# Two-layer block, its attention: on which queue the turned probabilities are read back from DRAM

## The chip, the core and the metric

The kernel runs on one core of one Trainium2 chip, in one launch. The metric is the time of that launch on the device in microseconds, as the median of several runs. All data are float32.

## The reference, cut to what matters

The program computes two transformer-like layers over `x` of shape (4, 512, 512). Before each sublayer `x` goes through a gate, a bidirectional scan over the sequence (`bi_wkv`), and each sublayer's result is added to `x`. Layer 0 is a state-space mixer and a mixture of 8 experts, layer 1 an attention and a gated feed-forward net (FFN).

```python
x = x + mamba2(gate0(x));  x = x + moe(gate1(x))
x = x + attention(gate2(x));  x = x + ffn(gate3(x))

def attention(x, w_q, w_kv, w_dense):      # 16 heads in 4 groups, 128 channels each
    q = (x @ w_q).reshape(b, 512, 4, 4, 128)
    k, v = split(x @ w_kv)                 # one k and one v for each group of 4 heads
    s = einsum('bqgpd,bkgd->bqgpk', q, k) * 128 ** -0.5
    p = softmax(where(causal, s, -inf))
    ctx = einsum('bqgpk,bkgd->bqgpd', p, v)
    return ctx.reshape(b, 512, 2048) @ w_dense
```

## The kernel before

The kernel is written for a scheduling layer: the program states its operations in an order, the layer puts them on the engines' queues in an order of its own choice and adds the semaphores. `tc.issue_after(i)` ties what is written inside it behind instruction `i` in that order. The helper `after(*engines)` (L88) does that with the last instruction so far of each engine named.

Every queue works in its own order. TensorE runs matrix products; VectorE (DVE), ScalarE (ACT) and GpSimd (POOL) run elementwise work; SyncE (SP) only issues DMA transfers. A DMA is issued by one of the engines' queues. The issuing queue first waits for what the transfer needs, and whatever stands behind it on that queue waits too.

The attention runs over `heads_` (L1738): four groups `g`, in each four batches `b`, in each four heads `i`, so 64 heads. I count them 0 to 63 in that order; the four heads of one (`g`, `b`) are called first to fourth. For one head:

- `start_group` (L1585), once in four heads: `pk` (L1593) and `pv` (L1601) on TensorE, copied by ScalarE to `kT` (L1597) and `v` (L1609).
- `queries` (L1612): `pq` (L1615) on TensorE, scaled to `qT` (L1623) by ScalarE. `begin(n + 1)` writes it one head ahead.
- `scores` (L1626), for each of four blocks of 128 queries (`qi`): `psc` (L1637) on TensorE; mask (L1640) and negated maximum `nmax` (L1642) on VectorE; the exponential `pr` with its row sum on ScalarE (`act`, the helper's line L128); reciprocal and scaling (L1648, L1649) and `nc.vector.transpose` (L1653) on VectorE. That last turns each 32x32 square and writes it to `blocks`.
- `blocks` (one of two `turned` tiles) then lies with its 32x32 squares in the wrong places among the partitions. Four transfers on GpSimd's queue (L1661) write it to a DRAM buffer `d`, one of four in turn. One transfer (L1678, in `collect`) reads it back as `pT`, all squares in place: 128 partitions of 1,664 elements. `pT` has two buffers.
- `context` (L1682): `pctx` (L1703) on TensorE with `pT` and `v`, copied by ScalarE to `cx` (L1711). After the fourth head `dense` (L1714) runs `pd` (L1718) and adds to `x` on VectorE (L1726).

The loop (L1757) holds three heads back: `context` of head n - 3 is written after `scores` of head n. `collect(1)` is called in `scores`, ahead of the first block (L1635). It reads back the blocks of all heads but the newest one written. So the readback of head n - 2 is written at the start of head n's scores, behind `qT` of head n + 1. `collect()` within `context` takes what is left; that happens only for head 61, since heads 62 and 63 are turned on TensorE (`ptp`, L1690) and do not go through DRAM. 62 heads are read back.

Beside the heads VectorE and ScalarE compute gates for later sublayers, in pieces. `nudge` (L390) steps that generator, four times a head, under `with after(nc.vector, nc.scalar)` (L1643). The gates' inputs come on SyncE's queue: `kt` (L240), `ek` (L247), `ekv` (L249), and their results leave there (L344). Also on SyncE's queue are the experts' result rows `rr` (L1483, `combine`), the weights `wq`, `wkv`, `wd` (L1466, L1472, L1566) and the FFN's weights (L1834 to L1839). ScalarE's queue issues only the 16 output transfers of the FFN (L1828).

Of the kernel before, what the change touches and what calls it, by code (L numbers as in the profile page):

```python
# [83 lines left out]
def block_kernel(ctx: ExitStack, tc: tile.TileContext, a: dict, out: bass.AP):  # L84
    nc = tc.nc

    @contextmanager
    def after(*engines):  # L88

        with ExitStack() as es:  # L90
            for e in engines:
                last = next(
                    (i for i in reversed(nc.cur_bb.bb.instructions) if i.engine == e.engine), None
                )
                if last is not None:
                    es.enter_context(tc.issue_after(last))
            yield
# [1454 lines left out]
    with att as ph:  # L1552
# [73 lines left out]
        def scores(u, i, qT):  # L1626
# [5 lines left out]
            for qi in range(NT):  # L1632
                n = (qi + 1) * P
                if qi == 0:
                    collect(1)  # L1635
                psc = ps_mm("psc")
                nc.tensor.matmul(  # L1637
                    psc[:, :n], lhsT=qT[:, qi * P : n], rhs=u.kT[:, :n], start=True, stop=True
                )
                nc.vector.tensor_tensor(psc[:, qi * P : n], psc[:, qi * P : n], mask, ALU.add)  # L1640
                nmax = sm.tile([P, 1], F32, tag="nmax", name="nmax", bufs=4)
                nc.vector.tensor_reduce(nmax, psc[:, :n], AX.X, ALU.max, negate=True)  # L1642
                with after(nc.vector, nc.scalar):  # L1643
                    nudge()
                pr = sm.tile([P, n], F32, tag=f"pr{qi}", name="pr")
                rsum = sm.tile([P, 1], F32, tag="rsum", name="rsum", bufs=4)
                act(pr, psc[:, :n], AF.Exp, bias=nmax, accum_out=rsum)
                nc.vector.reciprocal(rsum, rsum)  # L1648
                nc.vector.tensor_scalar(pr, pr, rsum, None, ALU.mult)  # L1649
                if turn:  # L1650
                    prs.append(pr)
                    continue
                nc.vector.transpose(  # L1653
                    blocks[:, :, 3 * qi : 4 * qi + 1, :].rearrange("p c k j -> p k c j"), pr
                )
# [14 lines left out]
        def new_pT():  # L1670
            return sm.tile([P, QUAD, SLOTS, SQ], F32, tag="pT", name="pT")

        def collect(rest=0):

            while len(away) > rest:
                d = away.pop(0)
                back[id(d)] = pT = new_pT()
                nc.sync.dma_start(  # L1678
                    out=pT.rearrange("p r k j -> p (r k j)"), in_=d.rearrange("c i r s -> (c i) (r s)")
                )  # L1680

        def context(u, prs):  # L1682

            if isinstance(prs, list):
                pT = new_pT()
                for qi, pr in enumerate(prs):
                    n = (qi + 1) * P
                    ptp = ps_tp("ptp")
                    for kj in range(qi + 1):
                        nc.tensor.transpose(  # L1690
                            ptp[:, kj * P : (kj + 1) * P], pr[:, kj * P : (kj + 1) * P], ident
                        )
                    nc.any.tensor_copy(
                        pT[:, :, 3 * qi : 4 * qi + 1, :].rearrange("p r k j -> p k r j"),
                        ptp[:, :n].rearrange("p (k r j) -> p k r j", r=QUAD, j=SQ),
                    )
            else:
                if id(prs) not in back:
                    collect()
                pT = back.pop(id(prs))  # L1700
# [86 lines left out]
    with ExitStack() as ph:  # L1787
# [48 lines left out]
        for lo, hi in ((0, 4), (4, 8), (8, NFF)):  # L1836
            nc.sync.dma_start(
                out=wdn[:, lo:hi, :],
                in_=ffd_d[lo * P : hi * P, :].rearrange("(i p) m -> p i m", p=P),  # L1839
# [44 lines left out]
        with tc.If(n_odd > 0):  # L1884
            with ExitStack() as gen:
                wl = gen.enter_context(tc.tile_pool(name="ff_gen", bufs=2, **right))
                for b in range(B):
                    h = gated(3, b, x[b], gp, tag="h", name=f"h4_{b}")
                    hd = []
                    for i in range(NFF):  # L1890
                        cs = slice(i * P, (i + 1) * P)
                        pv = []
                        for name in ("gateT", "upT"):
                            w = wl.tile([P, NC, P], F32, tag=name, name=name)
                            nc.sync.dma_start(
                                out=w, in_=a[name][:, cs].rearrange("(k p) m -> p k m", p=P)
# [13 lines left out]
                    for m in range(NC):  # L1910
                        w = wl.tile([P, NFF, P], F32, tag="downT", name="downT")
                        nc.sync.dma_start(
                            out=w,
                            in_=a["downT"][:, m * P : (m + 1) * P].rearrange("(i p) m -> p i m", p=P),
# [76 lines left out]
```

## Time and profile before

| what | value |
|---|---|
| runs shown | 2270.66, 2264.39, 2270.62 us, median 2270.62 |
| the profiled execution | 2262.92 us, of which the span is 2260.9 |
| granted TensorE clock in it | 0.983 of full speed |
| TensorE busy | 2123.0 us, 94% of the span |
| VectorE busy | 1524.8 us, 67% |
| ScalarE busy | 971.5 us, 43% |
| GpSimd busy | 418.4 us, 19% |
| readback issues (L1678) | 62 on SyncE's queue, 832 KB each, from 1171.4 to 1972.4 us |
| write issues (L1661) | 248 on GpSimd's queue, 208 KB each, 4.0 us from issue to landing (median) |

The profile is one execution with a record of each instruction's start and length and of each DMA packet. The span goes from its first instruction to its last; the profiled execution's own time is 2.0 us longer. Some engines wait beside others' work, so a wait counts only where it stands on the path to the end. A wait is put down to what ended it. "SPq" and "ACTq" are the queues of SyncE and ScalarE, where issuing a DMA is not counted as busy time. The attention's heads lie between some 1143 and 2003 us.

### The profile page before, as it was taken

The page shows a single profiled execution, that of the slowest core. Times are in us where ns is not written, and L with a number is a line of the kernel's source. Part 1 is how long each engine was busy: PE and PEld are TensorE (multiplying, and loading weights), DVE is VectorE, ACT ScalarE, POOL GpSimd, SP SyncE. Part 2 cuts the span into 40 slices and gives each one's busy share as a digit, 9 for nine tenths or more (in the row PEclk, how much of TensorE's full clock was granted, in tenths as well). Part 3 has the DMA queues.
Part 4 walks back from the last instruction along what each step waited for, and adds up shares of the span by engine and source line. Part 5 has one row for each costly group of instructions (what it writes and reads, how often), then busy time and mean ns, then how long its engine had stood idle before and what let it go on. Part 6 is the DMA issues. An engine that isn't in the chain of part 4 may idle for free.

```text
span 2260.9 us, 23897 instructions
## 1 busy us (share of the span) xinstructions
PE 2123.0 (94%) x7528; PEld 1219.8 (54%) x7528; DVE 1524.8 (67%) x3040; ACT 971.5 (43%) x1901; POOL 418.4 (19%) x558
## 2 busy tenths in 40 slices
PE   2879999999999999999989999999999999999998
PEld 1545565555655444444444555545555555568887
DVE  8698989989643665566577767677767765465332
ACT  4476676766732234333154433333334333243221
POOL 4023242321331111211211111111111111100000
PEclk9889999999999999999989999999999999999999
DMA  7542241531523548978666555455545464441100
GB/s 261 174 141 75 95 166 66 169 111 63 193 71 135 192 159 297 352 261 292 210 238 206 177 181 168 140 164 185 169 151 164 147 196 133 148 158 38 38 19 20
DMA packets 112455, 357.38 MB, mean 158 GB/s; under 512 B 14595, under 2 KB 23171, under 8 KB 102915
## 3 DMA queue, kind: packets, MB, share of 16 engines
q1 hardware_dynamic: 87584, 277.26, 36.1%
q0 software_dynamic: 22432, 74.34, 11.0%
q10 hardware_dynamic: 2304, 4.20, 0.5%
q8 instruction: 62, 1.02, 0.2%
q14 instruction: 73, 0.57, 0.1%
HBM read 337.91 MB, written 108.00 MB: 197 GB/s over the span
## 4 chain that ended last, share of the span: by engine, by line
PE 36%; DVE 9%; DMA 2%; ACT 2%; issue 1%; SPq 0%; DVEq 0%; ACTq 0%
PE pd L1718 9%; PE pq L1615 5%; PE pctx L1703 3%; PE psc L1637 3%; PE pk L1593 3%; PE pv L1601 3%; PE pfo L1821 2%; PE pfo L1820 2%; PE pfg L1820 2%; PE pfg L1821 2%; PE pfu L1821 2%; PE pfu L1820 2%; DVE turned L1653 2%; DVE nmax L1642 2%; DMA pT<-turned 1%; DVE pr L1649 1%
## 5 line engine op out<-in xcount | busy, mean ns | idle before, releaser
L1661 POOL DMA_DIRECT2D turned<-turned x248 | 135.2, 552 | 701.2 <-DVE turned L1653 399.0
L1615 PE MATMUL pq<-h,wq 128*128 128x512 f32 x512 | 230.9, 593 | 2.2 <-DVE h L404 1.7
L1718 PE MATMUL pd<-cx,wd 128*128 128x512 f32 x512 | 224.0, 593 | 1.9 <-ACT cx L1711 1.6
L128 ACT ACTIVATE pr<-psc,nmax 128x128 f32<-128x128 f32 (+3 forms) x256 | 134.6, 526 | 166.1 <-DVE nmax L1642 165.4
L1048 PE MATMUL pc<-h,wxb 128*128 128x512 f32 x320 | 148.5, 620 | 42.8 <-DVE h L1307 38.9
L1640 DVE TENSOR_TENSOR psc<-psc,mask 128x128 f32<-128x128 f32 x256 | 70.7, 284 | 144.3 <-PE psc L1637 144.3
L1637 PE MATMUL psc<-kT,qT 128*128 128x128 f32 (+3 forms) x512 | 156.3, 442 | 12.0 <-ACT pr L128 12.0
L1718 PEld LDWEIGHTS pd<-cx,wd 128*128 128x128 f32 x512 | 95.6, 190 | 118.5 <-issue 108.1
L1703 PE MATMUL pctx<-pT,v 128*128 128x512 f32 (+3 forms) x512 | 149.7, 434 | 9.9 <-DMA pT<-turned 9.6
L1703 PEld LDWEIGHTS pctx<-pT,v 128*128 128x128 f32 x512 | 96.6, 190 | 90.2 <-issue 61.1
L1615 PEld LDWEIGHTS pq<-h,wq 128*128 128x128 f32 x512 | 92.6, 190 | 96.3 <-issue 90.8
L811 PE MATMUL pg<-w,hT 128*128 128x512 f32 x296 | 136.6, 603 | 6.8 <-ACT hT L784 6.8
L844 PE MATMUL po<-w,yT 128*128 128x512 f32 x296 | 135.9, 600 | 6.2 <-ACT yT L837 6.2
L822 PE MATMUL pn<-w,hT 128*128 128x512 f32 x296 | 133.4, 593 | 0.0
L1048 PEld LDWEIGHTS pc<-h,wxb 128*128 128x128 f32 x320 | 61.9, 198 | 115.8 <-issue 73.8
L1642 DVE TENSOR_REDUCE nmax<-psc 128x1 f32<-128x128 f32 (+3 forms) x256 | 122.7, 482 | 2.1
L1637 PEld LDWEIGHTS psc<-kT,qT 128*128 128x128 f32 x512 | 85.9, 192 | 70.5 <-ACT pr L128 26.9
L1726 DVE TENSOR_TENSOR xr<-xr,pd 128x512 f32<-128x512 f32 x64 | 43.5, 680 | 117.7 <-PE pd L1718 117.7
L1653 DVE STREAM_TRANSPOSE turned<-pr 128x128 f32<-128x128 f32 x248 | 120.7, 498 | 1.8
L1119 PE MATMUL pz<-wzt,h 128*128 128x512 f32 x256 | 115.2, 599 | 0.3 <-ACT st L1220 0.3
L1267 PE MATMUL po<-wot,yT 128*128 128x512 f32 x256 | 114.2, 600 | 0.0
L811 PEld LDWEIGHTS pg<-w,hT 128*128 128x128 f32 x296 | 56.2, 194 | 75.9 <-issue 66.3
(343 smaller groups left out, 4172.9 us busy)
## 6 DMA issues: line engine op xcount, KB each, us to landing
w<-in_w1x SPq DMA_DIRECT2D x76, 1024.0 KB
turned<-turned POOLq DMA_DIRECT2D x248, 208.0 KB, 4.0
pT<-turned SPq DMA_DIRECT2D x62, 832.0 KB
w<-in_w2x SPq DMA_DIRECT2D x38, 1024.0 KB
wb<-in_b1x SPq DMA_DIRECT2D x38, 512.0 KB
lm<-cs SPq DMA_DIRECT2D x32, 512.0 KB
kt<-in_fT SPq DMA_DIRECT2D x62, 256.0 KB
ek<-ek SPq DMA_DIRECT2D x62, 256.0 KB
```

The costliest lines, as they stand in the source:

```text
L811: nc.tensor.matmul(pg, lhsT=hT[:, k, :], rhs=self.w1[s][0][:, k, :], start=(k == 0), stop=(k == NC - 1))
L844: nc.tensor.matmul(po, lhsT=yT[:, j, :], rhs=self.w2[s][:, j, :], start=(j == 0), stop=(j == NI - 1))
L1048: nc.tensor.matmul(pc, lhsT=wxb[:, k, m * P : (m + 1) * P], rhs=h[:, k, :], start=(k == 0), stop=(k == NC - 1),)
L1615: nc.tensor.matmul(pq, lhsT=u.wq[:, k, i * KVC : (i + 1) * KVC], rhs=u.h[:, k, :], start=(k == 0), stop=(k == NC - 1),)
L1637: nc.tensor.matmul(psc[:, :n], lhsT=qT[:, qi * P : n], rhs=u.kT[:, :n], start=True, stop=True)
L1642: nc.vector.tensor_reduce(nmax, psc[:, :n], AX.X, ALU.max, negate=True)
L1653: nc.vector.transpose(blocks[:, :, 3 * qi : 4 * qi + 1, :].rearrange("p c k j -> p k c j"), pr)
L1661: nc.gpsimd.dma_start(out=d[:, :, r].rearrange("c i s -> i c s"), in_=blocks[r * SQ : (r + 1) * SQ].rearrange("i c k j -> i c (k j)"),)
L1703: nc.tensor.matmul(pctx[:, kj * P :].rearrange("p (q r j) -> p q r j", r=QUAD, j=SQ), lhsT=u.v[:, kj, :], rhs=pT[:, :, 4 * kj : 10 + kj : ...
L1718: nc.tensor.matmul(po, lhsT=dense_w[u.g][:, i, m * P : (m + 1) * P], rhs=u.ctxT[i], start=(i == 0), stop=(i == HPG - 1),)
L1820: nc.tensor.matmul(out_, lhsT=w, rhs=xs[0], start=first_, stop=False)
L1821: nc.tensor.matmul(out_, lhsT=w, rhs=xs[1], start=False, stop=last_)
```

## The change

The readback in `collect` is issued on ScalarE's queue in place of SyncE's, and it is written under `after(nc.scalar)`, that is, tied behind the last instruction that was written for ScalarE before it. The bytes moved, the buffers and the writes on GpSimd's queue are the same. Lines below it move down by two.

```diff
             while len(away) > rest:
                 d = away.pop(0)
                 back[id(d)] = pT = new_pT()
-                nc.sync.dma_start(
-                    out=pT.rearrange("p r k j -> p (r k j)"), in_=d.rearrange("c i r s -> (c i) (r s)")
-                )
+                with after(nc.scalar):
+                    nc.scalar.dma_start(
+                        out=pT.rearrange("p r k j -> p (r k j)"),
+                        in_=d.rearrange("c i r s -> (c i) (r s)"),
+                    )
```

A DMA issued on ScalarE's queue is an instruction of ScalarE to `after`. The `nudge` that follows `collect` in the first block of a head is therefore tied behind the readback's issue, where before it was tied behind `qT` or a later ScalarE instruction.

## The prediction

> **What bounds the kernel now.** The page comes first. Its profiled execution took 2262.92 us, 2260.9 of them span. The runs shown have a median of 2270.62 (2264.39 to 2270.66), so I work out a difference against the profiled execution and add it to the median. A measurement of this kernel can tell about 0.3% (6.8 us) from no change.
>
> ```profile
> span 2260.9 us, 23897 instructions
> PE 2123.0 (94%) x7528; PEld 1219.8 (54%) x7528; DVE 1524.8 (67%) x3040; ACT 971.5 (43%) x1901; POOL 418.4 (19%) x558
> ```
>
> TensorE is the bound; ScalarE is less than half busy. Second, the table by stretches of the span, for the attention (columns: length; PE, PEld, DVE, ACT, POOL busy with counts; granted clock; DMA share; GB/s):
>
> ```profile
> 1120.00:1300.00 180.00, 161.47 (x552) 87.24 (x553) 129.71 (x309) 83.77 (x173) 28.84 (x54) 0.96 0.65 205
> 1300.00:1600.00 300.00, 289.20 (x926) 154.51 (x924) 213.27 (x556) 118.50 (x283) 50.05 (x92) 1.00 0.56 169
> 1600.00:2010.00 410.00, 405.04 (x1308) 218.88 (x1309) 250.02 (x686) 141.52 (x354) 61.01 (x113) 1.00 0.52 166
> ```
>
> TensorE is idle for 18.5 + 10.8 + 5.0 = 34.3 us of the 890. No change to the attention alone can win more than that, and after 1600 us almost nothing is left. Third, the chain of waits, TensorE's in the attention and SyncE's own in the whole span:
>
> ```profile
> PE psc L1637 <- ACT pr L128: 12.0, 12, 3.2
> PE pctx L1703 <- DMA pT<-turned: 9.6, 4, 3.3
> ...
> SPq L240 <- DVE eu L278: 243.0, 38, 20.5
> SPq L1678 <- DMA turned<-turned: 146.9, 40, 9.1
> ...
> SPq L1678 <- PE pctx L1703: 104.6, 11, 20.0
> ```
>
> The readback (L1678) reaches TensorE's clock by 9.6 us in 4 waits. The 251.5 us that SyncE stands at it cost nothing in themselves. They could only hurt through what is queued behind them, the gate loads (L240, L247, L249), and no engine's wait for those loads stands among TensorE's or VectorE's waits in the attention.
>
> Fourth, the timeline around the longest of the four waits, head 19 (heads count from 0 in the loop's order), SyncE, then ScalarE, then TensorE:
>
> ```profile
> 1429.26 0.33 SPq L240 DMA_DIRECT2D kt<-in_fT  x1
> 1429.81 0.82 SPq L1678 DMA_DIRECT2D pT<-turned  x1
> ...
> 1430.22 0.58 ACT L128 ACTIVATE pr<-psc,nmax 128x384 f32<-128x384 f32 x1 [0.42 <-DVE nmax L1642]
> ...
> 1438.07 2.39 PE L1703 MATMUL pctx<-pT,v 128*128 128x512 f32 x8 [3.31 <-DMA pT<-turned]
> ```
>
> The written blocks of head 19 had landed at 1424.9, but the readback was issued only at 1429.81, just behind a gate load that had waited for a buffer. It landed 7.8 us later, and TensorE lost 3.31. The other three waits look the same (heads 15, 23, 31: a gate load 0.56 us ahead in the queue). This is what the change goes for.
>
> **The removed part.** 62 issues of 0.32 us and their waits leave SyncE's queue. Gate, weight and row loads behind them start earlier. I price that at nothing: TensorE's waits that a load could shorten in the attention are `pcb` behind `rr` (4.4 us, 5 times), and those rows were held by a buffer that `pcb` itself frees. The FFN's weights leave the readbacks behind too and start before 1972 us, but TensorE has no wait for them to lose; their DMA then runs beside the last readbacks, which have 2 to 5 us to spare.
>
> **The added part: issuing on ScalarE.** The nearest row is the output's DMA, the one kind that ScalarE issues before:
>
> ```profile
> 2058.71 0.60 ACT L1806 CAST h_hi<-h 128x512 fp32r<-128x512 f32 x1
> 2058.83 0.38 ACTq L1828 DMA_DIRECT2D out<-ot  x1
> 2059.43 0.63 ACT L128 ACTIVATE th<-xr 128x512 f32<-128x512 f32 x1
> ```
>
> The issue goes out 0.12 us after the cast ahead of it starts, 0.48 before that cast ends, and the next instruction starts 0.12 after the cast's end (2058.71 + 0.60 = 2059.31). So an issue that need not wait costs ScalarE 0.12 us, or 0.34 where nothing covers it: 62 x 0.12 = 7 us, at most 62 x 0.34 = 21 us, on an engine that is idle for 546 of these 890 us. On the path only the 12 waits of TensorE for `pr` count: 12 x 0.12 = 1.4 at the low end, 12 x 0.34 = 4 at the high; below nothing too if the new order shortens them. I take +1.
>
> **The added wait.** ScalarE now stands at a readback until the head's four writes have landed. Queued behind it are the exponentials, `qT`, `kT`, `v` and `cx`, for which TensorE waits. For each of the 62 I took the ScalarE instruction that stands just ahead in the new built order, and compared its end in this trace with the landing of the last write. In 59 cases the writes had been down for 1.6 us or more before the issue. In the other three (heads 1, 13, 25) they are 0.7, 2.1 and 9.7 us short, but for 13 and 25 ScalarE's next TensorE-bound work, `kT`, starts only some 16 us later. Price: 0; from above, 3 us.
>
> [...]
>
> **The moved part: when the readback is issued.** The tie puts it behind the last ScalarE work written before it. In this trace's times that is a median of 4.2 us later than SyncE issued it, and 17 to 24 us later for most second heads of a group. What that costs, readback by readback: arrival is the end of the ScalarE instruction ahead less 0.48 (or the writes' landing, if later), plus the time this readback took in the trace from issue to its last 6,656-byte packet (3.9 to 8.5 us, median 5.1). Need is the start of its `pctx`, less its wait of before, plus the TensorE work that the new order puts ahead of it. Slack by place in the group of four:
> - first heads: 6 to 22 us. Dense and the next group's `pk`, `pv` lie between.
> - second heads: 1.3 us or more, but for head 61. That one is collected inside `context`, so behind `cx` of head 60: 1.8 short, with 2.9 us of transposes put between.
> - third heads: 3.1 or more, but for head 2 (0.5 short) and head 6 (0).
> - fourth heads: here it fails. Short are head 3 by 2.8, 15 by 1.5, 19 by 3.3, 23 by 2.7, 27 by 2.7, 31 by 2.9, 35 by 0.2, together 16.1.
>
> The sum is 16.1 + 1.8 + 0.5 = 18.4 us of waits, where 9.6 stood: +8.8. That keeps each transfer as slow as it was. The other end takes them at the undisturbed 4.1 us (head 51 issued at 1852.1, landed 1856.2): then short are only head 3 by 1.2, 27 by 0.3, 31 by 1.0, 61 by 1.9, in all 4.4, which is -5.2. The truth lies between. The gate load that ran just ahead on SyncE's queue now has a queue of its own, but the next head's writes (2.2 us of the 16 DMA engines beside head 19) stay. I take the middle, 11.4, so +1.8.
>
> [...]
>
> **Order on the other engines.** In the built order TensorE's rows stay in place but for some four dozen moves (`pq`, `pk` and the first `pctx` earlier or later by one to four matmuls); VectorE has several hundred, mostly gate scans against `nmax` and `rsum`, because the gate work is tied to the last ScalarE instruction, now a DMA. GpSimd's order is the same. VectorE waits for TensorE (144.3 us at `psc`), not the other way, after 1300 us. Before that, TensorE's 18.5 idle us can move either way; I take 0 and keep 5 on both sides.
>
> **The sum.** +1.8 waits for `pT`, +1 ScalarE, 0 the rest: 2262.9 + 2.8 = 2265.7 for a profiled execution like this one, and 2270.62 + 2.8 = 2273.4 for the median. I say 2273.5.
>
> **The rivals.**
> - Slower: the transfers stay as slow as they were on SyncE's queue, and fourth heads pay in full. +8.8, with ScalarE's high end 4 and its late landings 3: 2279 to 2287. For it: the later issue is in the built order, and the writes still overlap. Against it: one of the two causes of slow transfers is gone. It decides where a fourth head's readback takes over about 5 us. Chance 0.28.
> - Much slower: ScalarE becomes the head of the line. If VectorE's new order makes the last transposes of a head 5 us later, the 1.6 to 10 us by which fourth heads' writes precede are gone, and the exponentials behind stop: 15 fourth heads by 2 us and more, 2290 to 2310. Against it: 59 of 62 with margin. Chance 0.08.
> - Faster: all waits for `pT` fall (-9.6), and part of the early idle time, up to 5 us: 2257 to 2264. For it: four waits behind a gate load, which vanish in kind. Against it: ScalarE reaches the readback no earlier than SyncE did. Chance 0.22.
> - About the same, the forecast: 2263 to 2279. Chance 0.42.
>
> The range 2259 to 2288 leaves out the much slower case and the tails of the outer two. Faster by over 0.3% (under 2263.8) is the faster case: 0.22. Slower (over 2277.4) is the two slower cases and a little of the forecast: 0.38. Within 0.3%: 0.40.
>
> **What would show it.** TensorE's wait `pctx <- DMA pT<-turned` at 8 to 15 us in 6 to 9 waits, all at fourth heads and head 61; ScalarE's DMA rows of 0.34 us without long idle ahead of the next exponential; 4 to 6 us from issue to landing. If that wait is under 3 us, the faster rival holds; over 18, the slower. If `pr` waits for DMA, or TensorE's wait for `pr` goes well beyond 12.0, ScalarE is the head of the line. If the stretch 1120 to 1300 moves by over 5 us, the orders of VectorE and TensorE decided, which I priced at nothing.

## The result, and the profile after

The changed kernel takes 2287.34 us (median of 10 runs, 2280.01 to 2291.92) where the kernel before took 2269.18 (10 runs beside them, 2261.4 to 2277.68). The ratio is 1.0078, with a 95% interval of 1.0064 to 1.0092: slower by 18.2 us. The profiled execution took 2286.27 us, 1.1 below its median; that of before, 2262.92, lies 6.3 below its own. The head of the page after, and its chain of work that ended last, by engine:

```profile
span 2284.5 us, 23902 instructions
PE 2138.2 (94%) x7528; PEld 1230.4 (54%) x7528; DVE 1527.0 (67%) x3041; ACT 970.2 (42%) x1900; POOL 416.3 (18%) x558
...
PE 37%; DVE 8%; DMA 4%; ACT 1%; issue 1%; ACTq 0%; DVEq 0%; SPq 0%
```

TensorE's instruction count is the same, and its busy time is 15.2 us longer for those 7528 matmuls. The table by stretches has the first reason in its clock column:

```profile
1120.00:1300.00 180.00, 159.47 (x524) 84.82 (x523) 131.98 (x314) 84.41 (x174) 27.89 (x52) 0.95 0.66 212
1300.00:1600.00 300.00, 287.43 (x928) 155.34 (x927) 197.78 (x508) 107.08 (x259) 45.87 (x84) 0.98 0.53 161
1600.00:2010.00 410.00, 402.36 (x1284) 216.18 (x1283) 260.01 (x719) 141.98 (x360) 67.76 (x124) 1.00 0.53 160
```

Between 1300 and 1600 us the granted clock was 1.00 before and is 0.98 now. The chain of waits in the attention has the second reason (columns: total, times, longest). TensorE first, then SyncE:

```profile
PE pctx L1705 <- DMA pT<-turned: 25.4, 13, 5.6
PE psc L1637 <- ACT pr L128: 8.2, 7, 3.2
...
SPq L1836 <- DMA pT<-turned: 121.4, 5, 65.5
```

The wait for `pT` went from 9.6 us in 4 to 25.4 in 13. The wait for `pr` fell from 12.0 to 8.2: ScalarE did not become the head of the line. The last line is new, and harmless: it is SyncE's queue at the FFN's weight loads, and the FFN takes the same 265 us from its first matmul to the end.

The issue itself is as cheap as its nearest row said (ScalarE's line of the readback: count, then min, median and max in ns):

```profile
L1679 ACTq DMA_DIRECT2D pT<-turned x62: 326/326/347, 1183.4 to 2010.4; - x62
```

**Where the 23.6 us between the two spans lie.** Up to the attention's first `pk`: +9.6 us, ahead of the first instruction that the change touches. From there to the FFN's first matmul: +13.8. After that: +0.2. The 13.8 are 8.5 more idle time of TensorE (+15.8 for `pT`, -7.3 for everything else) and 5.3 more busy time at a lower clock. The clock's record in this stretch has 23.9 us at 0.5 after, 6.8 before (a dip that lies across the first `pk` in both is left out); the new dips begin at 1211, 1348, 1559 and 1781 us, at the waits for `pT` of 3.29, 2.42, 5.56 and 2.52 us: the third 2.8 us before its wait ends, the others within 1 us behind theirs. The stretch around the third, then the one after it, in the changed kernel:

```profile
1559.00:1566.00 7.00, 4.13 (x5) 1.85 (x6) 3.61 (x12) 0.81 (x3) 2.18 (x4) 0.51 1.01 377
1566.00:1576.00 10.00, 10.00 (x27) 4.79 (x26) 6.54 (x17) 3.04 (x8) 0.00 (x0) 1.00 0.38 119
```

The 9.6 us upstream are the clock: up to the first `pk` every engine that computes runs the same instructions in the same order in both traces, the clock's record has 83.5 us at 0.5 after and 63.2 before, and TensorE's busy time is 9.7 us longer. The two profiled executions stand 5.2 us further apart than the two medians, so part of this is the execution that was caught. Over the 14 kernels profiled in this study the attention began between 1131.3 and 1141.8 us. no_writes (experiment 4), faster than the kernel before, began at 1140.1 with 84.0 us at 0.5. What of it the change brings about is open.

### The profile page after: what moved, and what is told of

Its sections match the earlier page's. It is cut to its first block, busy times and chain, and to the rows that moved or that the text cites. A ratio compares the mean times of both kernels' runs of the same rounds, so it can differ in the third digit from the quotient of the medians.

```text
span 2284.5 us, 23902 instructions
## 1 busy us (share of the span) xinstructions
PE 2138.2 (94%) x7528; PEld 1230.4 (54%) x7528; DVE 1527.0 (67%) x3041; ACT 970.2 (42%) x1900; POOL 416.3 (18%) x558
## 4 chain that ended last, share of the span: by engine, by line
PE 37%; DVE 8%; DMA 4%; ACT 1%; issue 1%; ACTq 0%; DVEq 0%; SPq 0%
PE pd L1720 9%; PE pq L1615 5%; PE pctx L1705 4%; DMA pT<-turned 3%; PE psc L1637 3%; PE pv L1601 3%; PE pk L1593 2%; PE pfo L1823 2%; PE pfo L1822 2%; PE pfg L1822 2%; PE pfg L1823 2%; PE pfu L1823 2%; PE pfu L1822 2%; DVE nmax L1642 1%; DVE turned L1653 1%; DVE pr L1649 1%
## 5 line engine op out<-in xcount | busy, mean ns | idle before, releaser
L1705 PE MATMUL pctx<-pT,v 128*128 128x512 f32 (+3 forms) x512 | 155.3, 444 | 25.5 <-DMA pT<-turned 25.4
```

Of the source, the lines that this page charges most:

```text
L1705: nc.tensor.matmul(pctx[:, kj * P :].rearrange("p (q r j) -> p q r j", r=QUAD, j=SQ), lhsT=u.v[:, kj, :], rhs=pT[:, :, 4 * kj : 10 + kj : ...
```

## The experiments

A head's place in its group of four is called first to fourth, as in the prediction. A readback's time is from its issue to its last 6,656-byte packet; its need is the start of its `pctx` less the wait there.

**1. The tie alone, and the queue alone.** The change has two parts, so each was run without the other.

```
     # tie_sync: the tie, but SyncE issues
     with after(nc.scalar):
-        nc.scalar.dma_start(
+        nc.sync.dma_start(
     # scalar_free: ScalarE issues, no tie
-    with after(nc.scalar):
+    if True:
         nc.scalar.dma_start(
```

> The tie alone: the readback stays behind ScalarE's last work in the built order, but SyncE issues it. Theory A (the loss comes from the readback's place in ScalarE's own in-order queue): TensorE's waits for pT in the attention return to about 10 us (from 25.4), no dip of the granted clock after 1250 us, ratio to the kernel before 1.000, between 0.997 and 1.003. Rival B (the tie itself makes the readback late, whoever issues it): waits of 20 us or more, ratio 1.006 to 1.009. Rival D (the loss is in the changed order of VectorE and TensorE, not in the waits for pT): waits near 10 us and yet a ratio over 1.004.

> The queue alone: ScalarE issues the readback, with no tie. Theory A: the readback still stands in the order of ScalarE's queue, so fourth heads stay late; TensorE's waits for pT 18 us or more, dips of the granted clock behind them, ratio 1.005 to 1.009. Rival B (the tie is the cause): waits under 12 us, ratio 0.998 to 1.003. Issue to landing stays at a median of 5 us under both.

Measured: tie_sync 1.0003 (0.9986 to 1.0019), waits for `pT` 9.0 us in 4; scalar_free 0.9987 (0.9968 to 1.0006). TensorE's wait in tie_sync, then in scalar_free:

```profile
PE pctx L1705 <- DMA pT<-turned: 9.0, 4, 3.3
...
PE pctx L1705 <- DMA pT<-turned: 12.0, 6, 3.4
```

So neither part costs anything measurable alone. Rival B (the tie) falls with the first. Theory A as stated (the place in ScalarE's queue) falls with the second: there the fourth heads' readbacks are issued just as late against their need, 5.8 us on average against 5.6 in the changed kernel, and yet the loss is gone. tie_sync had two dips that its expectation ruled out, at 1441 and 1608 us, at the waits of heads 19 and 31 (3.31 and 2.29 us), which had none in the kernel before (3.31 and 2.55): a dip at a wait is not certain. The two dips, 10.2 us at 0.5, went with 4.8 us more busy time of TensorE in the attention for the same matmuls in the same order. So part of the changed kernel's 5.3 may belong to the execution that was caught. With SyncE issuing, the tie moves nothing on the engines that compute: the built order of TensorE, VectorE and ScalarE is that of the kernel before, row for row. On ScalarE's own queue it does move things.

**2. Later and earlier on ScalarE's queue.**

```
     # act_late: in scores()
-    if qi == 0:
+    if qi == 2:
         collect(1)
     # act_early: taken out of scores(), and in the loop over heads
     if len(held) > 3:
         settle()
+    collect(1)
```

> The changed kernel, but the readback is collected at the third row block (qi == 2) of a head instead of at the first, tied to ScalarE's last work as before: later in ScalarE's order by up to three instructions, some 2 to 6 us. Theory A: third and fourth heads come later, waits for pT 45 us or more, more dips of the clock, ratio 1.012 to 1.03. Rival D (the waits are a symptom, the order on VectorE is the cause): ratio within 0.004 of the changed kernel's 1.008.

> The changed kernel (ScalarE's queue, with the tie), but the readback is collected right after the head's settle() instead of at the next head's first row block, so it is tied to cx and no longer to the qT behind it: up to 4 us earlier for third heads, little for fourth heads, which stand behind pr or cx either way. If place in ScalarE's order is the cause: third heads 2, 6 and 10 stop waiting or wait as in the run without the tie (3.4 us), waits for pT in all 10 to 17 us (from 25.4), ratio 0.999 to 1.004. If the tie in itself costs (whatever it is tied to): waits 22 us or more, ratio 1.006 to 1.010.

Measured: act_late 1.0153 (1.0129 to 1.0176), waits 37.4 us in 18, of which third heads 20.8 (changed kernel 6.1) and fourth heads 15.3 (18.6); act_early 1.0023 (1.0009 to 1.0037), waits 13.8 in 9, third heads 0.6, fourth heads 12.6. Time follows these waits in both directions. act_late's ratio was as expected, its waits fell short of the 45: third heads were issued 6.3 us ahead of their need instead of 8.6, and second heads 7.4 instead of 11.9, but fourth heads 5.6 as in the changed kernel. Rival D, by which the loss does not pass through these waits, falls with it.

**3. Whose tie is it?** The tie was given to the readbacks of some places only, all 62 on ScalarE's queue.

```
-    collect(1)
+    collect(1, i)
     ...
-    with after(nc.scalar):
+    with after(*((nc.scalar,) if i == 1 else ())):    # tie_fourth
     # tie_rest: i != 1    tie_second: i == 3    tie_third: i == 0
```

> ScalarE's queue, the tie for fourth heads only (the collecting head has i == 1); the other 47 readbacks have none. If the fourth heads' own tie makes them pay: fourth heads wait 15 us or more, ratio 1.005 to 1.008. If it is the tie of the other heads that moves VectorE's work and so the next head's writes into the fourth heads' readbacks: fourth heads take about 5.1 us and wait under 11 us, ratio 0.998 to 1.003.

> The complement: ScalarE's queue, the tie for all but fourth heads. If the fourth heads' own tie makes them pay: waits for pT 9 to 14 us with third heads in front, ratio 0.999 to 1.004. If the tie of the others does it through the order on VectorE: fourth heads take about 6 us and wait 15 us or more, ratio 1.005 to 1.008.

> ScalarE's queue, the tie for second heads only (collecting head i == 3). In the changed kernel they were issued 16 us after their landing instead of at once, and their readbacks cost TensorE no wait themselves. If moving them is what brings the next group's first writes into the fourth heads' readbacks: fourth heads 27, 35 and 43 wait 2 us or more each as in the changed kernel, waits for pT 18 us or more, ratio 1.004 to 1.007. If it is the third heads' tie: waits under 13 us, ratio 0.997 to 1.002.

> ScalarE's queue, the tie for third heads only (collecting head i == 0), which puts them behind qT instead of cx and in the changed kernel brought their issue from 12.9 to 9.5 us before the need. If it is the third heads' tie that counts: head 6 waits 2.8 us, fourth heads 27, 35 and 43 wait 2 us or more each, waits for pT 18 us or more, ratio 1.004 to 1.008. If it is the second heads': waits under 14 us, ratio 0.998 to 1.003. Should both kernels lie between (1.002 to 1.004, waits 14 to 18 us each), the two ties share the loss.

Measured, with the 15 fourth heads (3 to 59) apart; "beside" is the time that packets of the neighbouring heads' writes took during the head's readback, summed over the 16 DMA engines and divided by 16, in us:

| kernel | ratio (95%) | waits for `pT`, us | fourth: issue to need | readback | beside | waits |
|---|---|---|---|---|---|---|
| before | 1 | 9.6 | 8.8 | 5.70 | 1.27 | 9.6 |
| scalar_free | 0.9987 (0.9968 to 1.0006) | 12.0 | 5.8 | 5.15 | 0.94 | 8.8 |
| tie_fourth | 0.9984 (0.9964 to 1.0003) | 11.8 | 5.6 | 5.08 | 0.79 | 8.6 |
| tie_second | 1.0027 (1.0011 to 1.0043) | 18.0 | 5.9 | 5.86 | 1.43 | 14.9 |
| tie_third | 1.0064 (1.0040 to 1.0088) | 30.0 | 5.5 | 6.23 | 1.86 | 22.6 |
| tie_rest | 1.0055 (1.0035 to 1.0074) | 26.6 | 5.8 | 6.18 | 1.84 | 19.0 |
| changed | 1.0078 (1.0064 to 1.0092) | 25.4 | 5.6 | 6.02 | 1.65 | 18.6 |

It is not the fourth heads' own tie: without it the loss stays, with it alone there is none. In the built order, TensorE's rows of tie_rest are those of the changed kernel without exception, and tie_fourth's are scalar_free's but for 72 places of 7528. The third heads' tie is enough for most of the loss, the second heads' for about a third (heads 27 and 43, which its expectation named, did not wait there; others did). The ties of the other heads move work on VectorE, and with it the time at which the next head's blocks are written: GpSimd issues those writes 1.0 us behind VectorE's last transpose in all these kernels (median), and in the changed kernel they begin 8.9 us ahead of the fourth head's need, in scalar_free 10.3 (medians). The sharing that follows is seen at head 27 in the changed kernel (timeline: GpSimd's four writes of head 28; ScalarE with the readback; TensorE):

```profile
1550.28 2.18 POOL L1661 DMA_DIRECT2D turned<-turned  x4 [8.49 <-DVE psc L1640]
...
1552.17 0.47 ACT L128 ACTIVATE pr<-psc,nmax 128x256 f32<-128x256 f32 x1 [1.12 <-DVE nmax L1642]
1552.33 0.33 ACTq L1679 DMA_DIRECT2D pT<-turned  x1
...
1561.87 2.04 PE L1705 MATMUL pctx<-pT,v 128*128 128x512 f32 x2 [5.56 <-DMA pT<-turned]
```

The readback goes out 2.05 us behind the writes' first issue and shares the engines with them. The DMA queues while it ran, 1552.3 to 1561.2 (q10 is ScalarE's queue, q0 carries the writes, q1 the loads on SyncE's queue):

```profile
q0 software_dynamic: 213, 0.66, 34.9%
q10 hardware_dynamic: 142, 0.85, 34.2%
q1 hardware_dynamic: 331, 0.91, 25.4%
```

The same readback in scalar_free, 1544.7 to 1549.9:

```profile
q10 hardware_dynamic: 141, 0.85, 66.7%
q0 software_dynamic: 73, 0.28, 13.3%
```

The same bytes took 8.9 us in the first and 5.2 in the second. Head 27 is also issued later against its need in the changed kernel, 4.0 us ahead of it instead of 7.6, so it shows lateness and sharing together. Over the 15 fourth heads an estimate tells them apart. In the traces a readback made TensorE wait when its last packet plus some 0.5 us lay behind the need (0.39 to 0.66 us from that packet to `pctx` in the 17 waits of the kernel before and the changed one). The changed kernel's issue times with its own readback times give 18.5 us by that; with scalar_free's readback times 9.5. scalar_free's issue times give 8.7 with its own readback times and 16.9 with the changed kernel's. So the longer readbacks make 8 to 9 us of the difference, the later issue 1 to 2. The loads on q1 took 0.8 us beside a fourth head's readback in the changed kernel and 0.7 in scalar_free (means, counted as "beside" is), so they don't make the difference between these two.

**4. Take the writes away.** If that sharing is the cause, the changed kernel without the neighbours' writes must lose its loss, with the readbacks issued as late as ever.

```
-    for r in range(QUAD):
+    for r in range(QUAD if i or (u.g, u.b) == (0, 0) else 0):
         nc.gpsimd.dma_start(
```

> The changed kernel without the four writes of the first head of each group of four (from the second group on), so that the fourth heads' readbacks run beside no writes; the readback of a first head then brings in old probabilities. If the writes of the next head are what makes the fourth heads' readbacks slow: they take 4.2 to 5.0 us from issue to landing (mean 6.0 in the changed kernel), heads 11, 27, 31, 35 and 43 wait under 1 us each, waits for pT in all 6 to 12 us (from 25.4), ratio 0.998 to 1.003. If something else makes them slow (the queue itself, the gate loads): they stay at 5.5 us or more, waits over 18 us, ratio 1.005 or more.

A first head's readback then brings in old probabilities, so only the run's time is used. Measured: 0.9976 (0.9966 to 0.9987). Fourth heads: issue to need 5.7 us on average, as before the edit (head 27's is 6.6 instead of 4.0); readback 4.63 (from 6.02), none over 5.4; waits 2.4 us (from 18.6). Heads 2, 6 and 61 wait about as they did: they are issued 2.5 to 3.8 us ahead of their need, and no readback of this run took under 3.9. TensorE's wait, and the queues beside head 27's readback (1545.5 to 1550.8, 5.3 us):

```profile
PE pctx L1705 <- DMA pT<-turned: 9.6, 8, 3.3
```

```profile
q10 hardware_dynamic: 143, 0.85, 58.5%
q1 hardware_dynamic: 111, 0.42, 23.3%
```

q0 is gone from the list. Gate loads and weights (q1) are still there, 0.5 us beside a fourth head's readback on average. Where more of them meet a readback they make it late too: head 47's in scalar_free took 7.2 us beside 3.1 us of q1 and 0.5 of writes, and TensorE waited 2.5. The run shows the cause at the fourth heads: readbacks issued 5.7 us ahead of their need (mean) cost 2.4 us of waits with the next head's writes gone (4.63 us each), and 18.6 us where they met those writes, issued 5.6 ahead (6.02 each). The run also leaves out issues on GpSimd and a share of all DMA, and its built order differs in places (110 on TensorE), so the price of the sharing is read from the fourth heads' waits, 18.6 - 2.4 = 16.2 us, and not from the ratio. With the changed kernel's issue times the estimate above gives 5.0 us of waits instead of 2.4, so some 13.5 to 16.2.

**5. A third queue.** GpSimd issues the readbacks, with no tie: all of them, the fourth heads', or the fourth heads' from the second group of heads on.

```
-    nc.sync.dma_start(
+    nc.gpsimd.dma_start(                                # pool_free
+    (nc.gpsimd if i == 1 else nc.sync).dma_start(       # pool_fourth
+    (nc.gpsimd if fourth else nc.sync).dma_start(       # pool_later: fourth = i == 1 and u.g > 0
```

> A third queue: GpSimd issues the readback, no tie. GpSimd issues the writes too and is 19% busy, so it can issue as soon as they have landed. Theory A: no fourth head is issued more than 3 us after the landing, waits for pT under 8 us, ratio 0.993 to 1.001. Rival C (a queue of its own lets the readback collide with the next writes and the gate loads, so any queue but SyncE's is slower): waits of 15 us or more, ratio over 1.004. A second way to be slow: GpSimd stands at the landing (some 7 us per head) and the next head's writes and the gate's work on GpSimd come late; that shows as waits of GpSimd for DMA and as later landings of the writes.

> A version to beat both: the kernel before, with GpSimd issuing the fourth heads' readbacks alone and SyncE the others; no tie. All four waits for pT of before are fourth heads' behind a gate load on SyncE's queue, and with GpSimd issuing all 62 no head waited. Theory: waits for pT under 2 us, the early attention not delayed as with all 62 on GpSimd (there head 2 came 14 us later than head 0 did), ratio 0.993 to 0.997. Rival: GpSimd's stand at the landing delays its gate work or the next head's writes and gives it back: ratio 0.998 or more.

> The best version so far (fourth heads read back on GpSimd's queue, the others on SyncE's), but only from the second group of heads on (u.g > 0), which holds all four waits of before (heads 15, 19, 23, 31). If the early delay of GpSimd's work (head 3 came 8.8 us later there than head 0 did) is a loss: ratio 0.992 to 0.995. If it is given back by itself, as the later heads of that profile suggest: the same as that version, 0.994 to 0.998, waits for pT under 1 us.

Measured: 0.998 (0.9965 to 0.9996), 0.996 (0.9945 to 0.9975) and 0.9952 (0.9934 to 0.9969); no wait for `pT` in any of the three. Rival C, by which any queue but SyncE's is slower, falls with pool_free and scalar_free. pool_later has the lowest median of all, 2257.99 us where the kernel before had 2267.73 beside it. Its interval overlaps that of pool_fourth, so whether sparing the first group is worth anything stays open. Its stretches show TensorE idle for 4.6 us from 1300 to 1600 (10.8 before), at full clock:

```profile
1300.00:1600.00 300.00, 295.44 (x956) 158.76 (x955) 216.00 (x558) 119.76 (x287) 52.15 (x96) 1.00 0.56 169
1600.00:2010.00 410.00, 406.56 (x1311) 218.79 (x1310) 251.43 (x688) 146.07 (x361) 66.04 (x121) 1.00 0.54 167
```

The reason given in advance was wrong, though. GpSimd doesn't issue sooner (in pool_free a median of 4.5 us behind the landing for fourth heads, where at most 3 was expected), and its transfers take longer, a median of 7.7 us for the 12 fourth heads of pool_later where the kernel before had a mean of 5.70 for its 15 (the readback's lines in pool_later):

```profile
L1678 POOL DMA_DIRECT2D pT<-turned x12: 557/557/584, 1377.4 to 1955.2; - x12
...
DMA to landing us min/median/max: 7.2/7.7/9.3
```

Most of that is the neighbours again: 2.3 us of writes lay beside a fourth head's readback (1.3 before), and head 14's in pool_free, with none beside it, took 4.3 us on the same queue. What changed is the need. With the readback on GpSimd the built order puts a fourth head's `pctx` and the dense projection behind the next group's `pk`, `pv` and part of `pq`: from the last transpose of a fourth head to its `pctx` there are 25.3 us (median of heads 15 to 59) instead of 16.8. The 8.5 us pay for the slower transfer with some to spare.

**All kernels in one table.** "Attention" is from the first `pk` to the FFN's first matmul in the profiled execution, "half clock" what the clock's record has at 0.5 in it, "own" TensorE's busy time in it. Half clock leaves out, in every row, the dip that lies across the first `pk`.

| kernel | ratio | waits for `pT` | half clock, us | attention, us | own, us |
|---|---|---|---|---|---|
| pool_later | 0.9952 | 0 | 6.8 | 854.7 | 832.3 |
| before | 1 | 9.6 | 6.8 | 864.7 | 834.4 |
| scalar_free | 0.9987 | 12.0 | 13.7 | 862.4 | 836.1 |
| act_early | 1.0023 | 13.8 | 27.3 | 874.7 | 843.3 |
| changed | 1.0078 | 25.4 | 23.9 | 878.5 | 839.7 |
| tie_third | 1.0064 | 30.0 | 30.7 | 885.3 | 842.4 |
| act_late | 1.0153 | 37.4 | 41.0 | 896.5 | 846.3 |

From the kernel before to act_late the attention grows by 31.9 us: 27.8 are waits for `pT`, 11.9 are busy time that comes with 34.2 us more of half clock, and the other idle time shrinks by 7.8. pool_later's row can't be set beside the others to that precision: 14 more of the attention's last matmuls stand behind the FFN's first one there, and the rest takes 267.3 us instead of 264.9.

## Why the prediction was right or wrong

The measured 2287.34 lies in the range by 0.7 us. It is the first rival's outcome, slower, 0.3 us above that rival's 2287, and not the forecast's. That the range held is partly luck: the rival's top had 8.8 us of waits for `pT`, 4 for ScalarE's issues and 3 for late landings, while the waits alone measured 15.8 and the other two did not show up. The bounds of the small terms held; the bounds of the moved issue did not.

- **What bounds the kernel, removed issues, FFN:** right. TensorE is at 94% as before, SyncE's freed queue brought nothing, and the FFN is 0.2 us longer.
- **ScalarE's issue cost (+1) and the added wait (0):** right in kind. The issue's row measured 0.326 us, just under the high end's 0.34. TensorE's waits for `pr` fell by 3.8 instead of rising by 1 to 4; none of ScalarE's waits in the attention is for the writes, and no semaphore row ahead of a readback is over 38 ns.
- **The moved issue (+1.8, between -5.2 and +8.8): the term that was mis-sized.** It measured +15.8, above its high end: 25.4 us of waits, where 11.4 were taken and 18.4 stood at the slow end. By place, fourth heads took 18.5 (16.1 at the slow end), third heads 6.1 (0.5) and head 61 0.8 (1.8). Heads 2, 3, 6, 15, 19, 23, 27, 31, 35 and 61, named with 18.4 us between them, took 19.6 (15 none); heads 7, 11, 43 and 47, not named, the other 5.9. Four things are wrong in the working. The middle was taken for no better reason than lying between two ends. The argument for the low end, that a queue of its own frees the readback of the gate load ahead, was false in effect, since the median from issue to last packet is 5.2 us on ScalarE's queue and 5.1 on SyncE's; and the trace before spoke against it, for beside head 19 the writes took 3.1 us of the engines' time (q0 has 40.5% of 1429.81 to 1437.58) and not 2.2, all other loads 1.3. Third heads came later against their need than was worked out: head 2 was issued 2.5 us ahead of it and head 6 3.8, while their readbacks took 5.3 and 6.1. And the high end was none: it kept each readback's old duration, which had been measured beside the old neighbours. Head 27's went from 6.5 to 8.9 us.
- **Order on the other engines (0, with 5 either way):** the step behind the last one. Several hundred moved rows on VectorE were priced as TensorE's waiting for VectorE. They also set when GpSimd writes, and so what a readback meets on the DMA engines; experiments 3 and 4 show that this, far more than the lateness, separates the changed kernel from scalar_free at the fourth heads, where 9.8 of the 13.4 us of waits between the two lie (third heads: 2.7, all of it head 6, issued 3.8 us ahead of its need instead of 8.6).
- **What was not priced at all:** the clock. 5.3 us of the attention's 13.8 are TensorE's own work, longer at half clock around the new waits; how much of it another execution would have is open.
- **The rivals.** "Slower" gave as its decision point readbacks of over about 5 us in the fourth heads; they took 6.0. "Much slower", ScalarE as head of the line, did not occur. "Faster" died because three of the four old waits only changed their place in the list: heads 19, 23 and 31 still wait 4.3 us.
- **What would show it:** the line set at 18 us of waits for the slower rival was crossed (25.4), and the stretch 1120 to 1300 moved TensorE's busy time by 2.0 us, within the 5 (the program runs some 9.6 us later in it).

To the argument of a queue of its own the rows of experiment 3 speak: beside head 27 the readback on q10 had 34.2% of the 16 engines' time and the writes on q0 34.9%, in the same 8.9 us, so the new queue did not keep the writes off it. In the kernel before all 62 readbacks were on SyncE's queue; the nearest row there was head 19's, where the writes had 40.5% beside a readback that took 7.8 us. Read so, the sum would have stood at its slow end.

What stays open: why the clock was lower in the 9.6 us ahead of the attention, and, with it, why the medians differ by 18.2 us when the attention accounts for 13.8.

## What to carry to other kernels

When a transfer is moved in time, price it against its new neighbours: its old duration belongs to the old ones (head 27's went from 6.5 to 8.9 us), and an instruction order that shifts elsewhere can shift those too (here the next head's writes from 10.3 to 8.9 us ahead of a fourth head's need, scalar_free to the changed kernel). Before expecting a gain from another queue, look at who shares the DMA engines during the transfer: here ScalarE's queue did not end the sharing with the writes (1.27 us of them beside a fourth head's readback before, 1.65 after). And where a late operand stalls TensorE, add something for the clock behind the stall (here 5.3 us of TensorE's own work beside 15.8 more of waits, in one trace of each kernel), or move the consumer instead of the transfer: with 8.5 us of other matmuls ahead of `pctx` no readback was late, though it took longer (7.2 to 9.3 us in pool_later). No run here moved the consumer alone.

## What the runs showed of the hardware

- In the changed kernel, four waits of 2.4 to 5.6 us on TensorE came with 3.4 or 6.8 us at a granted clock of 0.5, and one of 2.8 (head 6) did not; in tie_second waits of 1.9 and 2.1 us did, and in the kernel before one of 3.3 did not. From the kernel before to act_late 34.2 us more of half clock go with 11.9 us more busy time of TensorE, to tie_sync 10.2 with 4.8; ahead of the attention, with the same instructions in the same order, the changed kernel's trace has 20.3 us more of half clock than that of before and 9.7 more busy time. That is 0.35 to 0.48 us for each us at 0.5.
- The readback of 832 KB on ScalarE's queue took 3.9 to 4.4 us in the changed kernel where under 0.2 us of writes lay beside it (21 of 62), and up to 9.6 (head 27 in act_late) beside the next head's writes. On GpSimd's queue it took 4.3 us with no writes beside it (head 14 in pool_free), and 7.3 on average at the 36 heads of that run with 2 us or more.
